# Attention scores of two rounds in one run of TensorE, and one pool of eight PSUM banks

## The chip, the cores and the metric

The kernel runs on one core of one Trainium2 chip. The metric is the device time of one execution in microseconds (us). Nine runs of the kernel before have a median of 1870.49 us (1860.73 to 1880.05).

A core has TensorE (matrix products; results go to PSUM), VectorE, ScalarE, GpSimd and SyncE, each with its own queue of instructions worked off in order. PSUM has eight banks; a bank holds 512 fp32 values on each of 128 partitions. In the profile the engines are called PE, DVE, ACT, POOL and SP; PEld is the loading of TensorE's stationary operand.

## The reference

One transformer block over x of shape (16, 512, 256): a layernorm, causal attention with 16 heads of 16 dimensions, a mixture of 32 experts of which each token uses 4, and a shared expert; all sums go onto x.

```python
xn = _layernorm(x)
q, k = _rope(xn @ Wq.T, xn @ Wk.T)                # 16 heads of 16
scores = einsum('bqhd,bkhd->bhqk', q, k) / sqrt(16)
attn = softmax(where(causal, -inf, scores))
att = einsum('bhqk,bkhd->bqhd', attn, v) @ Wo.T
topk = top_k(softmax(xn @ router_w.T + router_bias), 4)   # weights made to sum to 1
moe = sum over the 4 chosen experts of weight * down(silu(gate(xn)) * up(xn))
shared = silu(xn @ sgate.T) * (xn @ sup.T) @ sdown.T
out = x + att + moe + shared
```

## The kernel before

All engines follow one order that the program writes out by hand. The main loop (L1074) runs over **rounds** `r`. Sixteen batch items, two halves `p` of the heads and ten rounds each give 320 rounds; a second pass over the scores trails by `LAG` = 12 rounds, so that 332 rounds have scores. In each round the loop calls `cut` (L1087), then `scores` (L1089), then sends off finished stores, and then places other work: `fill` steps (shared expert, later the experts) by a running balance of estimated cost, with the round's fixed `events` between and behind them (projections of q, k and v, transposes, routing, the attention sums `values`, the output projection).

**The scores** are computed twice. The first pass (`sq`, queries times keys) only yields each row's maximum: VectorE adds the causal mask and takes the maximum in one instruction for each block and head (L835, into `top`). `maxima` (L861) later transposes these maxima and adds them to the queries, as two more rows of the contraction. The second pass (`sk`, keys times queries, 18 rows instead of 16) then yields scores that are already shifted; ScalarE takes the exponential (L843, into `pe`), GpSimd zeroes the triangle above the diagonal (`cut`, L849), and `values` (L870) multiplies `pe` with v.

A head's operands lie in its own strip of 32 partitions, so that four matmuls for four heads use four different row groups of the array and run side by side. Four heads `g` = 0..3 share one round pair: an even round does `sq` of heads 0 and 1 and `sk` of heads 2 and 3, the odd round after it the same block with the heads exchanged. Within a round the matmuls of `sq` and `sk` alternate (L825). Per head, every block entry of `BLOCKS_Q` and `BLOCKS_K` has 512 columns in all: 512, 384 + 128 or 256 + 256.

**PSUM:** `ps_q` and `ps_k` (L90, L91) hold one tile of two banks each, for `sq` and `sk`. The pool `psum` (L92) holds four tiles of one bank, which all other matmuls take in turn through `bank` (L145). A tile can be taken again when all that read it are done. So `sq` of a round waits for the maxima of the round before, and `sk` for its exponential.

**Other names** in the prediction, with their lines: `psgu` and `psd` are the two matmul stages of the shared expert (L246, L258), `pg` and `py` those of the routed experts (L656, L680), `pxt` the transpose of an expert's rows (L643). Behind `psgu` and `pg` stands `glu` (L276): tanh on ScalarE, then two VectorE instructions, the last reading of the bank. Behind `pg` come the small VectorE instructions `four`, `wrow` and `who` (L666 to L674). `plt` and `pr` (L423, L459) belong to routing: `choose` and `rank` put a chain of some twenty small VectorE instructions behind them, and ScalarE copies `pr` to `ranks` (L461) only after its exponential of `wt` (L442), which waits for that chain. `pqk` is the projection of q and k (L755), `po` the product with v (L875), `place` (L521) VectorE's work that finds the rows of the expert blocks.

**Stages:** rounds 0 to 33 compute the routing; 34 to 129 scatter rows to the experts' blocks, with shared-expert steps as fill; 130 to 301 run the expert blocks as fill; from 302 on sums are combined and stored.

Of the kernel before, what the change touches and what calls it, by code (L numbers as in the profile page):

```python
# [11 lines left out]
F32 = mybir.dt.float32  # L12
# [10 lines left out]
P = 128  # L23
# [49 lines left out]
def block_kernel(ctx: ExitStack, tc, x, wqkv, wo, rope, rw, rb, wexp, sg, su, sd, out):  # L73
# [16 lines left out]
    ps_q = ctx.enter_context(tc.tile_pool(name="ps_q", bufs=1, space=PSUM))  # L90
    ps_k = ctx.enter_context(tc.tile_pool(name="ps_k", bufs=1, space=PSUM))  # L91
    psum = ctx.enter_context(tc.tile_pool(name="psum", bufs=4, space=PSUM))  # L92
# [52 lines left out]
    def bank(shape, name):  # L145
        return psum.tile(shape, F32, tag="m", name=name)
# [77 lines left out]
    def shared_steps(b, i2, late, sums, xt=None):  # L224
# [27 lines left out]
        def down():  # L252
            hold["py"] = bank([P, 2, D], f"psd_{name}")
            down_half(0)

        def down_half(il):
            for m in range(HS // P):
                nc.tensor.matmul(  # L258
                    hold["py"][:, il, :], lhsT=hold["h"][:, m, il * P : (il + 1) * P],
                    rhs=sd_sb[:, m, :], start=(m == 0), stop=(m == HS // P - 1),  # L260
                )
            if il == 0 and late:
                hold["xr"], *parts = hold["parts"]
                for part in parts:
                    nc.vector.tensor_tensor(hold["xr"], hold["xr"], part, ALU.add)
            if il == 1:
                nc.vector.tensor_tensor(hold["xr"], hold["xr"], hold["py"], ALU.add)
                stores.append((half(out_v if late else moe_v[0], b, i2), hold["xr"]))
# [4 lines left out]
            [down, lambda: down_half(1)],  # L273
# [526 lines left out]
    def scores(r):  # L800

        jobs = []
        if r < ROUNDS:
            b, s = divmod(r, 20)
            p, s = divmod(s, 10)
            g0 = 0 if s % 2 == 0 else 2
            sq = ps_q.tile([P, 2, S], F32, tag="q", name=f"sq_{r}")
            jobs.append([
                (sq[:, h, col : col + (i + 1) * P],
                 qts[b][(g0 + h) * HP : (g0 + h) * HP + DH, 2 * p + c, i * P : (i + 1) * P],  # L810
                 kts[b][(g0 + h) * HP : (g0 + h) * HP + DH, 2 * p + c, : (i + 1) * P])
                for c, i, col in BLOCKS_Q[s // 2] for h in range(2)
            ])
        if r >= LAG:
            bk, sk = divmod(r - LAG, 20)
            pk, sk = divmod(sk, 10)
            k0 = 2 if sk % 2 == 0 else 0
            st = ps_k.tile([P, 2, S], F32, tag="k", name=f"sk_{r}")
            jobs.append([
                (st[:, h, col : col + S - k * P],  # L820
                 kts[bk][(k0 + h) * HP : (k0 + h) * HP + DH + 2, 2 * pk + c, k * P : (k + 1) * P],
                 qts[bk][(k0 + h) * HP : (k0 + h) * HP + DH + 2, 2 * pk + c, k * P :])
                for c, k, col in BLOCKS_K[sk // 2] for h in range(2)
            ])
        for n in range(max(len(job) for job in jobs)):  # L825
            for job in jobs:
                if n < len(job):
                    dst, lhsT, rhs = job[n]
                    nc.tensor.matmul(dst, lhsT=lhsT, rhs=rhs, start=True, stop=True)  # L829
        if r < ROUNDS:  # L830
            for c, i, col in BLOCKS_Q[s // 2]:
                n = (i + 1) * P
                for h in range(2):
                    at = (g0 + h) * HP + DH + c
                    nc.vector.tensor_tensor_reduce(  # L835
                        out=junk[:, :n], in0=sq[:, h, col : col + n], in1=causal[:, S - n :],
                        scale=1.0, scalar=LOWEST, op0=ALU.add, op1=ALU.max,
                        accum_out=top[p][i][:, at : at + 1],
                    )
        if r >= LAG:  # L840
            j = sk // 2
            pe = work.tile([P, 2, S], F32, tag="pe", name=f"pe_{r}", bufs=8)
            nc.scalar.activation(pe, st, AF.Exp, scale=DH ** -0.5)  # L843
            uncut.append((pe, j))
            pes[bk, pk, j, k0 // 2] = pe
# [3 lines left out]
    def cut():  # L849


        for pe, j in uncut:
            for _, _, col in BLOCKS_K[j]:
                diag = pe[:, :, col : col + P]
                nc.gpsimd.affine_select(  # L855
                    out=diag, in_=diag, compare_op=ALU.is_ge, fill=0.0, base=0,
                    pattern=[[0, 2], [1, P]], channel_multiplier=-1,
                )
        uncut.clear()
# [10 lines left out]
    def values(b, p, c):  # L870
        po = bank([P, S], f"po_{b}_{p}_{c}")
        for k in range(NT):
            j, col = PLACE_K[c, k]
            for g in range(4):
# [3 lines left out]
                    rhs=pes[b, p, j, g // 2][:, g % 2, col : col + S - k * P],  # L878
# [195 lines left out]
    for r in range(last):  # L1074
# [12 lines left out]
        cut()  # L1087
        if r < ROUNDS + LAG:
            scores(r)  # L1089
# [63 lines left out]
```

## Time and profile before

| | |
|---|---|
| median of nine runs | 1870.49 us |
| the profiled execution, time | 1871.53 us |
| the profiled execution, span of its instructions | 1869.8 us |
| mean granted TensorE clock | 0.976 |
| instructions in the profile | 37883 |
| DMA, mean rate | 186 GB/s |

All steps of the prediction are added to the profiled execution's own time, 1871.53 us; 1.7 us of it lie outside the span. It stands 1.0 us above the median.

The profile's "busy" counts an engine as busy while any instruction is under way. Where an engine idles, the profile names what ended the wait (the releaser). The chain of waits is followed back from the last instruction. Each fp32 matmul shows as two passes, each a weight load and a matmul record, so a matmul of 512 columns appears twice. The end of a matmul is modelled, so starts are safer to compare than ends.

### The profile page before, as it was taken

Reading aid. Unit: us, or ns where it says so; the run is one execution under the profiler, and the core shown is the slowest. Engines: PE = TensorE matmul, PEld = TensorE weight load, DVE = VectorE, ACT = ScalarE, POOL = GpSimd, SP = SyncE. Lnnn points to the kernel's source line nnn. Section 1 sums busy time; section 2 is a strip of 40 time slices with the busy share of each in tenths; the row PEclk is TensorE's granted clock in tenths of the full one; section 3 lists DMA queues with packets and bytes.
Section 4 is the critical chain, followed back from the end, with each engine's and each line's share of the span. In section 5 each row is a group of like instructions: output and inputs, shape, how many; then the busy total and the mean of one; then the engine's idle time right before and its main releaser. Section 6 shows DMA issues by size and latency. Waiting matters only on the chain.

```text
span 1869.8 us, 37883 instructions
## 1 busy us (share of the span) xinstructions
PE 1773.0 (95%) x13361; PEld 1255.4 (67%) x13361; DVE 1223.5 (65%) x4243; ACT 839.3 (45%) x1481; POOL 1013.2 (54%) x1338
## 2 busy tenths in 40 slices
PE   8999998989888899999999999999999999999898
PEld 6765665656555556677777777777777777777555
DVE  6888885655655655566666667566665756666585
ACT  3345532333333333345555555555555555555432
POOL 3333416667657677525565565656565665665421
PEclk9999999899989999999999999999999999999999
DMA  4454443435444343357989798898989889897498
GB/s 161 163 179 152 162 146 131 155 119 184 138 157 155 109 149 104 129 162 202 237 195 244 191 233 225 199 236 199 242 196 232 218 205 239 191 249 164 107 304 277
DMA packets 227518, 347.97 MB, mean 186 GB/s; under 512 B 22656, under 2 KB 165760, under 8 KB 227328
## 3 DMA queue, kind: packets, MB, share of 16 engines
q1 hardware_dynamic: 167424, 260.29, 44.0%
q0 software_dynamic: 55296, 76.86, 21.0%
q10 hardware_dynamic: 4608, 8.39, 1.3%
q8 instruction: 106, 1.74, 0.4%
q14 instruction: 84, 0.69, 0.1%
HBM read 218.12 MB, written 128.39 MB: 185 GB/s over the span
## 4 chain that ended last, share of the span: by engine, by line
PE 78%; DVE 13%; DMA 4%; issue 2%; another core or an unknown queue 1%; ACT 1%; SPq 1%; POOL 0%; DVEq 0%; ACTq 0%; POOLq 0%
PE sq L829 15%; PE pg L656 14%; PE psgu L246 9%; PE py L680 7%; PE po L875 7%; PE pqk L755 5%; PE psd L258 4%; DVE junk L835 4%; PE pxt L643 4%; PE pt L793 3%; PE pv L783 3%; PE pa L923 2%; PE pot L891 1%; PE sk L829 1%
## 5 line engine op out<-in xcount | busy, mean ns | idle before, releaser
L835 DVE CUSTOM_DVE_ANT_0 junk<-sq,causal 128x256 bf16<-128x256 f32 (+3 forms) x1024 | 501.6, 490 | 282.3 <-PE sk L829 176.4
L694 POOL DMA_INDIRECT moe<-yb,who x288 | 449.6, 1561 | 333.8 <-DMA moe<-yb,who 120.7
L843 ACT ACTIVATE pe<-sk 128x1024 f32<-128x1024 f32 x320 | 327.7, 1024 | 368.7 <-PE sk L829 324.5
L829 PE MATMUL sq<-kt,qt 16*128 16x384 f32 (+3 forms) x2048 | 375.9, 467 | 45.0 <-DVE top L835 41.0
L855 POOL TENSOR_SCALAR_AFFINE_SELECT pe<-pe 128x256 f32<-128x256 f32 x512 | 270.9, 681 | 246.8 <-ACT pe L843 234.5
L829 PE MATMUL sk<-qt,kt 18*128 18x512 f32 (+3 forms) x2048 | 375.6, 467 | 1.3 <-issue 1.3
L829 PEld LDWEIGHTS sq<-kt,qt 16*128 16x128 f32 x2048 | 178.0, 186 | 185.1 <-issue 65.4
L656 PEld LDWEIGHTS pg<-xbt,w 128*128 128x128 f32 x2304 | 272.2, 191 | 34.0 <-issue 16.6
L549 POOL DMA_INDIRECT xs<-rows,pos x256 | 250.4, 978 | 81.1 <-issue 80.2
L656 PE MATMUL pg<-xbt,w 128*128 128x128 f32 x2304 | 288.3, 278 | 0.2 <-ACT xbt L647 0.2
L829 PEld LDWEIGHTS sk<-qt,kt 18*128 18x128 f32 x2048 | 178.0, 186 | 10.1 <-issue 7.6
L281 DVE SCALAR_TENSOR_TENSOR gs_e<-th_e,pg 128x256 f32<-128x256 f32 x144 | 60.6, 421 | 164.5 <-ACT th_e L279 151.0
L875 PE MATMUL po<-pe,va 128*32 128x512 f32 (+3 forms) x2048 | 155.5, 443 | 5.7 <-POOL pe L855 4.5
L680 PE MATMUL py<-w,ht 128*128 128x256 f32 x576 | 153.4, 389 | 1.3 <-DVE four L666 0.9
L246 PE MATMUL psgu<-sxt,sg_sb 128*128 128x256 f32 x496 | 146.3, 419 | 2.3 <-issue 1.8
L688 ACT ACTIVATE yb<-py,wrow 128x256 f32<-128x256 f32 x288 | 121.0, 473 | 33.1 <-PE py L680 28.3
L246 PE MATMUL psgu<-sxt,su_sb 128*128 128x256 f32 x496 | 135.4, 397 | 0.3 <-issue 0.2
L258 PE MATMUL psd<-sd_sb,hs 128*128 128x256 f32 x512 | 130.9, 399 | 3.2 <-DVE hs L282 2.4
L875 PEld LDWEIGHTS po<-pe,va 128*32 128x32 f32 x2048 | 60.8, 111 | 108.2 <-issue 84.1
L755 PE MATMUL pqk<-wqkv_sb,axt 128*128 128x512 f32 x240 | 119.4, 622 | 4.5 <-issue 3.6
L246 PEld LDWEIGHTS psgu<-sxt,sg_sb 128*128 128x128 f32 x496 | 90.2, 199 | 49.6 <-issue 29.2
L279 ACT ACTIVATE th_e<-pg 128x256 f32<-128x256 f32 x144 | 55.2, 383 | 146.9 <-PE pg L656 135.8
(150 smaller groups left out, 2394.1 us busy)
## 6 DMA issues: line engine op xcount, KB each, us to landing
w<-in_wexp SPq DMA_DIRECT2D x288, 384.5 KB
xb<-xs SPq DMA_DIRECT2D x144, 265.0 KB
sum<-moe SPq DMA_DIRECT2D x48, 256.0 KB
xn_d<-xn SPq DMA_DIRECT2D x16, 530.0 KB
rows<-xn_d SPq DMA_DIRECT2D x16, 530.0 KB
xt_d<-xt ACTq DMA_DIRECT2D x32, 256.0 KB
sxt<-xt_d SPq DMA_DIRECT2D x31, 256.0 KB
xn<-in_x SPq DMA_DIRECT2D x15, 512.0 KB
```

What stands on the lines that cost most here:

```text
L246: nc.tensor.matmul(ps[:, u, :], lhsT=w[:, c, m * P : (m + 1) * P], rhs=hold["xt"][:, c, :], start=(c == 0), stop=(c == 1),)
L258: nc.tensor.matmul(hold["py"][:, il, :], lhsT=hold["h"][:, m, il * P : (il + 1) * P], rhs=sd_sb[:, m, :], start=(m == 0), stop=(m == HS // ...
L549: nc.gpsimd.indirect_dma_start(out=views[n % NVIEWS], out_offset=bass.IndirectOffsetOnAxis(ap=index, axis=0), in_=row, in_offset=None,)
L656: nc.tensor.matmul(pg[:, u, c * HB : (c + 1) * HB], lhsT=w[n][:, c, at : at + H], rhs=rows[:, dc, c * HB : (c + 1) * HB], start=(dc == 0), ...
L680: nc.tensor.matmul(py[:, c, :], lhsT=h[:, c * P : (c + 1) * P], rhs=w[n][:, c, 2 * D : 3 * D], start=True, stop=True,)
L694: nc.gpsimd.indirect_dma_start(out=moe[c], out_offset=bass.IndirectOffsetOnAxis(ap=at[:, c : c + 1], axis=0), in_=yb[:, c, :], in_offset=N ...
L755: nc.tensor.matmul(pqk, lhsT=axts[b][:, c, tok], rhs=wqkv_sb[:, c, : 2 * D], start=(c == 0), stop=(c == 1),)
L829: nc.tensor.matmul(dst, lhsT=lhsT, rhs=rhs, start=True, stop=True)
L835: nc.vector.tensor_tensor_reduce(out=junk[:, :n], in0=sq[:, h, col : col + n], in1=causal[:, S - n :], scale=1.0, scalar=LOWEST, op0=ALU.a ...
L843: nc.scalar.activation(pe, st, AF.Exp, scale=DH ** -0.5)
L855: nc.gpsimd.affine_select(out=diag, in_=diag, compare_op=ALU.is_ge, fill=0.0, base=0, pattern=[[0, 2], [1, P]], channel_multiplier=-1,)
L875: nc.tensor.matmul(po[g * HP : (g + 1) * HP, k * P :], lhsT=va[b % 2][k][:, 8 * p + 4 * c + g, :], rhs=pes[b, p, j, g // 2][:, g % 2, col ...
```

## The change

`scores` is called only in even rounds and does the work of two rounds: `sq` of all four heads, one bank for each head, then `sk` of all four heads, one bank each. All eight banks become one-tile slots of one pool; `Q_BANKS` (0 to 3) and `K_BANKS` (4 to 7) serve the scores, and the list `free_banks` says in which order the other work takes banks between two runs: Q0, K0, Q1, K1, K2, K3. K banks return to the end of the list, Q banks do not (`once`).

Directly behind the matmuls stand the exponentials and the row maxima of heads 0 and 1. Those of heads 2 and 3 are put off: the exponentials behind the first fill step, the maxima behind the second (or to the end of the round). An exponential now covers one head (512 columns) instead of two (1024), and a `cut` instruction four heads instead of two. The shared expert's `down` takes one bank and one VectorE addition for each half instead of one for both. The number and shapes of the matmuls and of the row maxima stay.

```diff
-    ps_q = ctx.enter_context(tc.tile_pool(name="ps_q", bufs=1, space=PSUM))
-    ps_k = ctx.enter_context(tc.tile_pool(name="ps_k", bufs=1, space=PSUM))
-    psum = ctx.enter_context(tc.tile_pool(name="psum", bufs=4, space=PSUM))
+    psum = ctx.enter_context(tc.tile_pool(name="psum", bufs=1, space=PSUM))
+    Q_BANKS, K_BANKS = range(4), range(4, 8)
+    free_banks = [*K_BANKS, *Q_BANKS]
+    once = set()
...
-    def bank(shape, name):
-        return psum.tile(shape, F32, tag="m", name=name)
+    def bank(shape, name, n=None):
+        if n is None:
+            n = free_banks.pop(0)
+            if n not in once:
+                free_banks.append(n)
+        return psum.tile(shape, F32, tag=f"bank{n}", name=name)
...
     def scores(r):
+        later = []
         if r < ROUNDS:
...
+            sq = [bank([P, S], f"sq_{r}_{g}", Q_BANKS[g]) for g in range(4)]
+            for c, i, col in BLOCKS_Q[s // 2]:
+                for g in range(4):
+                    nc.tensor.matmul(
+                        sq[g][:, col : col + (i + 1) * P],
...
         if r >= LAG:
...
+            st = [bank([P, S], f"sk_{r}_{g}", K_BANKS[g]) for g in range(4)]
+            for c, k, col in BLOCKS_K[sk // 2]:
+                for g in range(4):
...
+            pe = work.tile([P, 4, S], F32, tag="pe", name=f"pe_{r}", bufs=4)
+            def exponentials(heads):
+                for g in heads:
+                    nc.scalar.activation(pe[:, g, :], st[g], AF.Exp, scale=DH ** -0.5)
+            exponentials((0, 1))
+            later.append(lambda: exponentials((2, 3)))
...
+            row_maxima((0, 1))
+            later.append(lambda: row_maxima((2, 3)))
+        if r < ROUNDS:
+            free_banks[:] = [Q_BANKS[0], K_BANKS[0], Q_BANKS[1], *K_BANKS[1:]]
+            once.update(Q_BANKS)
+        else:
+            free_banks[:] = [*Q_BANKS, *K_BANKS]
+            once.clear()
+        return later
...
-        cut()
-        if r < ROUNDS + LAG:
-            scores(r)
+        if r % 2 == 0:
+            cut()
+            later = scores(r) if r < ROUNDS + LAG else []
...
             step()
             owed -= cost
+            if later:
+                later.pop(0)()
...
+        while later:
+            later.pop(0)()
```

More of the change, by code (lines that the diff above doesn't have):

```diff
@@ L250, in gate_up, with down @@
             glu(hold["h"][:, m, :], ps, f"s{name}_{m}")
[L252 to L256, printed above, removed]
+        def down(il):
+            py = bank([P, D], f"psd_{name}_{il}")
             for m in range(HS // P):
                 nc.tensor.matmul(
-                    hold["py"][:, il, :], lhsT=hold["h"][:, m, il * P : (il + 1) * P],
-                    rhs=sd_sb[:, m, :], start=(m == 0), stop=(m == HS // P - 1),
+                    py, lhsT=hold["h"][:, m, il * P : (il + 1) * P], rhs=sd_sb[:, m, :],
+                    start=(m == 0), stop=(m == HS // P - 1),
                 )
@@ L265, in down_half @@
                     nc.vector.tensor_tensor(hold["xr"], hold["xr"], part, ALU.add)
+            here = hold["xr"][:, il, :]
+            nc.vector.tensor_tensor(here, here, py, ALU.add)
             if il == 1:
-                nc.vector.tensor_tensor(hold["xr"], hold["xr"], hold["py"], ALU.add)
                 stores.append((half(out_v if late else moe_v[0], b, i2), hold["xr"]))
@@ L272, in shared_steps @@
             [lambda m=m: gate_up(m) for m in range(HS // P)],
-            [down, lambda: down_half(1)],
+            [lambda il=il: down(il) for il in range(2)],
         )
@@ L800, in scores @@
     def scores(r):
-        jobs = []
+        later = []
         if r < ROUNDS:
@@ L805, in scores @@
             p, s = divmod(s, 10)
[L806 to L813, printed above, removed]
+            sq = [bank([P, S], f"sq_{r}_{g}", Q_BANKS[g]) for g in range(4)]
[3 more added lines that the diff above has]
+                        sq[g][:, col : col + (i + 1) * P],
+                        lhsT=qts[b][g * HP : g * HP + DH, 2 * p + c, i * P : (i + 1) * P],
+                        rhs=kts[b][g * HP : g * HP + DH, 2 * p + c, : (i + 1) * P],
+                        start=True, stop=True,
+                    )
         if r >= LAG:
@@ L816, in scores @@
             pk, sk = divmod(sk, 10)
[L817 to L829, printed above, removed]
-        if r < ROUNDS:
[L831 to L845, printed above, removed]
+            st = [bank([P, S], f"sk_{r}_{g}", K_BANKS[g]) for g in range(4)]
+            for c, k, col in BLOCKS_K[sk // 2]:
+                for g in range(4):
+                    rows = slice(g * HP, g * HP + DH + 2)
+                    nc.tensor.matmul(
+                        st[g][:, col : col + S - k * P],
+                        lhsT=kts[bk][rows, 2 * pk + c, k * P : (k + 1) * P],
+                        rhs=qts[bk][rows, 2 * pk + c, k * P :],
+                        start=True, stop=True,
+                    )
@@ new lines, in scores, with row_maxima @@
+            pe = work.tile([P, 4, S], F32, tag="pe", name=f"pe_{r}", bufs=4)
[4 more added lines that the diff above has]
+            later.append(lambda: exponentials((2, 3)))
+            uncut.append((pe, sk // 2))
+            pes[bk, pk, sk // 2] = pe
+        if r < ROUNDS:
+            def row_maxima(heads):
+                for g in heads:
+                    for c, i, col in BLOCKS_Q[s // 2]:
+                        n = (i + 1) * P
+                        at = g * HP + DH + c
+                        nc.vector.tensor_tensor_reduce(
+                            out=junk[:, :n], in0=sq[g][:, col : col + n], in1=causal[:, S - n :],
+                            scale=1.0, scalar=LOWEST, op0=ALU.add, op1=ALU.max,
+                            accum_out=top[p][i][:, at : at + 1],
+                        )
+            row_maxima((0, 1))
+            later.append(lambda: row_maxima((2, 3)))
@@ L856, in cut @@
                     out=diag, in_=diag, compare_op=ALU.is_ge, fill=0.0, base=0,
-                    pattern=[[0, 2], [1, P]], channel_multiplier=-1,
+                    pattern=[[0, 4], [1, P]], channel_multiplier=-1,
                 )
@@ L877, in values @@
                     lhsT=va[b % 2][k][:, 8 * p + 4 * c + g, :],
-                    rhs=pes[b, p, j, g // 2][:, g % 2, col : col + S - k * P],
+                    rhs=pes[b, p, j][:, g, col : col + S - k * P],
                     start=(k == 0), stop=(k == NT - 1), skip_group_check=True,
```

## The prediction

> **What bounds the kernel now.** I read the page's busy times and groups first:
>
> ```profile
> PE 1773.0 (95%) x13361; PEld 1255.4 (67%) x13361; DVE 1223.5 (65%) x4243; ACT 839.3 (45%) x1481; POOL 1013.2 (54%) x1338
> PE 78%; DVE 13%; DMA 4%; issue 2%; another core or an unknown queue 1%; ACT 1%; SPq 1%; POOL 0%; DVEq 0%; ACTq 0%; POOLq 0%
> L829 PE MATMUL sq<-kt,qt 16*128 16x384 f32 (+3 forms) x2048 | 375.9, 467 | 45.0 <-DVE top L835 41.0
> ```
>
> PE sets the end. It idles 97 us, 45.0 of them ahead of `sq`, which waits for the maxima of the round before. Then by stage (rounds 0-33, 34-129, 130-301, 302-319); the columns are stretch, length, and busy time of PE, PEld, DVE, ACT and POOL, then clock, DMA share and GB/s:
>
> ```profile
> 32.60:263.30 230.70, 215.78 (x1474) 151.39 (x1473) 192.67 (x769) 101.31 (x219) 77.78 (x232) 0.96 0.47 155
> 263.30:798.10 534.80, 480.41 (x3182) 314.64 (x3180) 319.46 (x998) 172.57 (x261) 343.55 (x442) 0.94 0.43 142
> 798.10:1737.00 938.90, 935.49 (x7772) 697.28 (x7768) 605.58 (x2204) 510.50 (x921) 551.19 (x558) 1.00 0.84 211
> 1737.00:1808.50 71.50, 61.99 (x497) 38.32 (x496) 49.42 (x155) 27.48 (x39) 18.15 (x35) 0.98 0.66 195
> ```
>
> In the third stage, half of the time, PE has almost no gap: only less PE work helps there. In the first, DVE is 84% busy. Run by run on the timeline, the waits ahead of `sq` are 5.3, 34.1, 0.6 and 5.2 us in the four stages.
>
> What a run of scores costs PE, from the timeline of an undisturbed one:
>
> ```profile
> 600.25 1.89 PE L258 MATMUL psd<-sd_sb,hs 128*128 128x256 f32 x8
> 602.08 0.69 PE L829 MATMUL sq<-kt,qt 16*128 16x512 f32 x1
> 602.61 0.59 PE L829 MATMUL sq<-kt,qt 16*128 16x512 f32 x1
> 603.14 1.07 PE L875 MATMUL po<-pe,va 128*32 128x512 f32 x8
> ```
>
> Two passes of four heads side by side take 0.53 us each. Inside longer runs a pass starts 0.32 us after one of 384 columns, so 512 columns alone are 0.43. The first pass and the way out thus carry 0.10 us each. The start carries 0.10 too: `psd` and the run overlap by 0.06 us (602.14 against 602.08), where neighbours of one kind overlap by 0.16. A run costs 0.31 us above its 0.86 us of streaming, nearly the same in all undisturbed runs.
>
> **Part 1, half the runs.** 320 rounds with `sq` become 160 runs: 160 x 0.31 = **-50 us** (5, 15, 27 and 3 by stage). That assumes that `sq` to `sk` costs no more than block to block does now. The rule that weighs against it is in the Trainium skill, "TensorEngine Tiling (Array Packing)", PSUM Bottleneck: tiling makes TensorE faster but not the emptying of PSUM, which may become the bound. It has no price; part 3 prices that side from rows.
>
> **Part 2, the old wait.** `sq` no longer waits for maxima issued directly before: these get a whole cycle of some 11 us. **-40 us** (5.3 + 34.1 + 0.6; the fourth stage is left out, see part 5).
>
> **Part 3, the new wait.** The first tile taken after a run is Q0, the bank of `sq` head 0. PE works in order, so the first fill step, and all behind it, waits until DVE has done head 0's maxima. DVE works in order too, and what is left from the fill steps ahead of the run comes first. Call D the time from a run's first matmul to its first maximum. One run whose last fill step was `pg`:
>
> ```profile
> 1208.73 0.58 PE L829 MATMUL sq<-kt,qt 16*128 16x384 f32 x1
> 1209.31 0.42 DVE L281 SCALAR_TENSOR_TENSOR gs_e<-th_e,pg 128x256 f32<-128x256 f32 x1 [1.48 <-ACT th_e L279]
> 1209.76 0.42 DVE L282 SCALAR_TENSOR_TENSOR ht<-gs_e,pg 128x256 f32<-128x256 f32 x1
> 1210.10 0.91 DVE L666 SCALAR_TENSOR_TENSOR four<-xb,w 128x4 f32<-128x4 f32 x2
> 1211.28 0.54 DVE L835 CUSTOM_DVE_ANT_0 junk<-sq,causal 128x384 bf16<-128x384 f32 x1
> ```
>
> D is 2.55 us here, though the scores were there after 1.15. Head 0's maxima take 0.73 us (512 columns) to 0.93 (384 + 128), 0.85 in the mean, and PE follows 0.05 later, as ahead of `sq` now. Without the wait the fill would begin at 2 x 0.86 + 0.20 = 1.92 us. The wait is therefore D + 0.90 - 1.92 = **D - 1.02 us** a run. Its floor is 0.17, as no D is below 1.19.
>
> I took D of every even round, whose preceding steps the change keeps. Means by stage: 4.07 (17 runs), 2.71 (48), 1.51 (86), 1.41 (9); 2.14 over all.
>
> - Rounds 130-301: where `py` is the last step (30 runs) D is 1.22, where it is `pg` (23 runs) 2.09, a chain that the change leaves. 86 x 0.49 = **+42 us**.
> - Rounds 0-33: `choose` and `rank` stand last in odd rounds, so D is their chain:
>
> ```profile
> 141.29 0.48 PE L829 MATMUL sq<-kt,qt 16*128 16x256 f32 x1 [0.53 <-DVE top L835]
> 142.72 0.28 DVE L425 TENSOR_TENSOR lg<-plt,rb_sb 128x128 f32<-128x128 f32 x1
> 145.84 0.21 ACT L442 ACTIVATE wt<-wt 128x16 f32<-128x16 f32 x1 [2.92 <-DVE wt L439]
> 145.96 0.25 ACT L461 COPY ranks<-pr 128x128 f32<-128x128 f32 x1
> 146.93 0.41 DVE L835 CUSTOM_DVE_ANT_0 junk<-sq,causal 128x256 bf16<-128x256 f32 x1
> ```
>
>   D is 5.64. Before, the next round's work covered it; now PE stands. `pr` also holds a K bank until ScalarE copies it, 4.9 us into the run, so `sk` stands too, inside the same wait. 17 x 3.05 = **+52 us**. Of this stage's 9.6 us of other PE idle time I take back half, **-5**: some are waits behind the same chain.
> - Rounds 34-129: nine of the thirteen D above 3 stand behind an odd round that ends with `po`, 2 us of PE work that gives DVE nothing; what DVE still holds then is mostly the odd round's maxima (1.5 to 1.9 us), which now run earlier. I take 1.6 us for 32 runs, 2.5 where `place` falls in the even round (9 runs) and 3.0 where in the odd (7): mean 1.97, 48 x 0.95 = **+46 us**. Bounds: D = 1.5 gives 23, the whole 2.71 gives 81.
>
> Emptying the K banks ahead of `sk` costs nothing more while DVE is later. The second tile, K0, needs the exponential of head 0: some 0.6 us after `sk` (ScalarE's copies of 512 columns take 0.585). After a first step `pxt` (0.44 us) that is 0.15 late: 29 x 0.15 = **+4 us**. Should ScalarE be behind as well, this grows, at most by the 0.6 us in all 160 runs.
>
> **Part 4, the clock.** The longest wait of PE now shows what standing still costs (columns as above):
>
> ```profile
> 703.07 1.21 PE L829 MATMUL sq<-kt,qt 16*128 16x512 f32 x1 [3.98 <-DVE top L835]
> 702.00:703.00 1.00, 0.00 (x0) 0.00 (x0) 0.93 (x7) 0.00 (x0) 0.70 (x2) 0.79 0.37 136
> 703.00:704.00 1.00, 0.93 (x4) 0.52 (x8) 1.00 (x4) 0.00 (x0) 0.69 (x2) 0.50 0.17 59
> ```
>
> The clock fell to 0.50 and stayed there for 6 us, which cost 3.1 us; a stall of 3 us near 380 us cost 3.2 us at half clock, 1.6. Ten runs of the first stage have D above 4, so waits above 3 us: 10 x 1.6 = **+16 us**, up to 31. The Trainium skill, "TensorE: Matmul & The Clock Gate", Part 1, has the gate open again after some 3.4 us of work; by it the estimate would be 10 x 1.7 = 17 us, and the long case above contradicts it.
>
> **Part 5, the rest.** Two exponentials of 512 columns (at 0.585) stand for one of 1024 (1.024): 320 x 0.15 = 47 us more on ACT, which is 45% busy and idles 369 us ahead of them. Two additions of 256 columns behind `psd` (0.42 each, as `gs`) stand for one of 0.68: 32 x 0.16 = 5 us more on DVE, between fill steps. Without that cover both would be paid, 52 us. Half as many `cut` instructions of twice the width take POOL at most the 271 us they take now, and `po` waited only 4.5 us for them. The twelve rounds with `sk` alone become six runs (7 us less PE), and the nine waits of the fourth stage would be 9 x 0.39 = 4 us, but from 1785 us on the chain of waits goes through DMA (`sum` loads and stores): **0** here, between -7 and +4.
>
> **Sum:** -50 - 40 + 42 + 52 - 5 + 46 + 4 + 16 = +65, so 1871.5 + 65 = **1937 us**: by stage +53, -3, +18 and -3. The median stands 1 us below the profiled time, which I neglect.
>
> **Rivals.**
> 1. *DVE catches up* (faster). The odd round's maxima move ahead by half a round, and DVE starts each run with less behind it. Parts 1 to 3 balance at a mean D of 1.02 + 90 / 160 = 1.58 us (2.14 now); below it the kernel is faster. At 1.35: 160 x 0.33 - 90 = -37, **1834 us**. For: 47 of the 86 runs of the third stage have D under 1.25. Against: the chains behind `pg` and `rank` start only when PE ends the step, whatever DVE did before. Chance 0.13.
> 2. *No relief* (slower still). D in rounds 34-129 stays at 2.71 (+35) and the clock costs 3.1 us a wait (+15): **1987 us**, and more if K0 comes late. For: DVE-heavy bursts already cost 34 us there. Chance 0.17.
> 3. *The runs don't pay*: `sq` to `sk` drains the array as a change of kind does, and part 1 gives nothing, +50: 1987 us. Against: the block of 384 columns and the next of 128 follow each other without a gap now. Chance 0.04, in the range above.
> 4. *A wash*: relief in the second stage and short clock losses just balance, 1866 to 1877 us. Chance 0.06.
>
> The forecast, 1877 to 1975, has 0.60. Faster by over 0.3% (which is about what a measurement of this kernel tells from no change) 0.13, within it 0.06, slower 0.81. The range for eight in ten goes from 1866, leaving most of rival 1 out, to 1990.
>
> **What would show it.** Right: PE waits for DVE `top` in front of the first fill tiles (`psgu`, `pg`, `pxt`), some 0.5 us a run in the third stage and 3 us in the first; none ahead of `sq`; runs of 2.0 us; a first stage some 50 us longer with a lower clock. Wrong: waits there below 90 us in all, D in the first stage near 2, or PE waiting mainly for ACT or for a K bank ahead of `sk`.

## The result, and the profile after

The changed kernel takes 2087.53 us (median of 20 runs, 2077.03 to 2105.13); the kernel before, timed beside it, 1864.01 us (62 runs). The ratio is 1.1205, 95% interval 1.1183 to 1.1226: slower by 223.5 us, where +65 was forecast. The direction was right, the size far off, beyond the range's upper end of 1990.

The profiled execution (2085.22 us), from the page: busy times of the engines, the granted clock in 40 slices, the chain of waits, and the groups of the two score passes.

```profile
PE 1872.3 (90%) x13361; PEld 1356.3 (65%) x13361; DVE 1224.5 (59%) x4275; ACT 847.6 (41%) x1801; POOL 967.8 (46%) x1082
PEclk9888998888888889789999999999999999999999
PE 68%; DVE 18%; issue 4%; another core or an unknown queue 4%; DMA 3%; ACT 3%; SPq 0%; POOL 0%; DVEq 0%; ACTq 0%; POOLq 0%
L815 PE MATMUL sq<-kt,qt 16*128 16x128 f32 (+3 forms) x2048 | 228.1, 472 | 26.2 <-ACT oc L901 10.9
L828 PE MATMUL sk<-qt,kt 18*128 18x128 f32 (+3 forms) x2048 | 251.9, 471 | 36.7 <-ACT ranks L466 7.5
```

DVE does the work it did before, but holds 18% of the chain instead of 13%. PE is "busy" 99 us longer with the same matmuls, mostly because its clock is lower (86 of the 99, worked out below). By stage (rounds 0-33, 34-129, 130-301; columns as in the prediction):

```profile
32.90:316.80 283.90, 235.87 (x1473) 168.97 (x1473) 194.81 (x777) 102.81 (x239) 75.59 (x215) 0.87 0.38 126
316.80:958.80 642.00, 546.90 (x3186) 369.27 (x3184) 319.41 (x1015) 175.03 (x357) 326.00 (x365) 0.85 0.36 119
958.80:1947.80 989.00, 948.33 (x7772) 724.52 (x7768) 603.58 (x2205) 513.94 (x1093) 532.45 (x422) 0.99 0.80 201
```

Each stretch runs from the first `sq` matmul of its stage to that of the next. Against before they are longer by 53, 107 and 50 us, where +53, -3 and +18 were forecast. The first stage came out as worked; the second holds most of the miss. The waits, by waiting group and releaser (us in total, times, longest), first PE's, then ScalarE's and DVE's:

```profile
PE psgu L253 <- DVE top L850: 28.5, 15, 5.1
PE psd L262 <- DVE top L850: 17.5, 8, 5.1
PE pa L942 <- DVE qt L885: 13.7, 5, 4.4
PE sq L815 <- ACT oc L901: 10.9, 3, 5.0
ACT pe L838 <- remote: 69.6, 13, 8.8
ACT oc L901 <- remote: 43.2, 7, 9.8
DVE junk L850 <- remote: 29.4, 6, 7.4
```

The first two are the forecast wait for Q0. With all smaller ones, the waits for DVE `top` ahead of other tiles than `sq` come to 54 us, less than the 90 below which the prediction called itself wrong. The third and fourth were not forecast. "Remote" means that a release arrived just before the waiting instruction started, while no instruction ended then that could have sent it: in all these rows it is a release by PE. The same rows stand in the profile of before, and the prediction passed over them:

```profile
ACT oc L882 <- remote: 41.2, 7, 7.8
DVE junk L835 <- remote: 37.3, 8, 7.6
```

All of them lie in rounds 34 to 129. This is what one looks like in the changed kernel, on the timeline of round 90:

```profile
692.72 0.44 PE L894 MATMUL po<-pe,va 128*32 128x128 f32 x5 [0.82 <-issue]
694.18 0.38 PE L894 MATMUL po<-pe,va 128*32 128x128 f32 x2 [1.01 <-issue]
694.49 1.28 PE L815 MATMUL sq<-kt,qt 16*128 16x384 f32 x2
696.95 0.96 POOL L554 DMA_INDIRECT xs<-rows,pos  x1 [0.30 <-issue]
700.11 0.58 ACT L901 COPY oc<-po 128x512 f32<-128x512 f32 x1 [5.52 <-remote]
700.74 1.02 PE L815 MATMUL sq<-kt,qt 16*128 16x384 f32 x5 [4.98 <-ACT oc L901]
```

The last matmul of `po` is over by 694.6, yet ScalarE's copy of it starts at 700.11: it was released 5.5 us late. Before, `sq` and `sk` had banks of their own and went on meanwhile (behind a `po` for whose release ScalarE stood 7.8 us, PE waited 3.0, for the copy itself). Now `sq` needs the bank that `po` holds, and PE stands for 4.98 us. In two single microseconds behind it the core looks so (columns as by stage):

```profile
699.00:700.00 1.00, 0.00 (x0) 0.00 (x0) 0.00 (x0) 0.00 (x0) 0.00 (x0) 0.50 0.00 0
707.00:708.00 1.00, 1.00 (x3) 0.67 (x3) 0.00 (x0) 0.00 (x0) 0.84 (x3) 0.50 0.00 0
```

At 699 no engine and no DMA does anything; eight microseconds later PE still runs at half clock. Releases are not all that is late: inside `po`, at 692.72, PE stood for 0.82 us with no wait at all ("issue"). Such idle time of PE comes to 29.6 us in rounds 34 to 129, and to 16.1 in the kernel before.

### The profile page after: what moved, and what is told of

Same layout as the page of the kernel before. It is cut to its first block, busy times and chain, and to the rows that moved or that the text cites. A ratio compares the mean times of both kernels' runs of the same rounds, so it can differ in the third digit from the quotient of the medians.

```text
span 2083.5 us, 38577 instructions
## 1 busy us (share of the span) xinstructions
PE 1872.3 (90%) x13361; PEld 1356.3 (65%) x13361; DVE 1224.5 (59%) x4275; ACT 847.6 (41%) x1801; POOL 967.8 (46%) x1082
## 4 chain that ended last, share of the span: by engine, by line
PE 68%; DVE 18%; issue 4%; another core or an unknown queue 4%; DMA 3%; ACT 3%; SPq 0%; POOL 0%; DVEq 0%; ACTq 0%; POOLq 0%
PE psgu L253 11%; PE pg L661 11%; PE sk L828 7%; PE po L894 6%; PE sq L815 6%; PE psd L262 5%; PE py L685 5%; DVE junk L850 5%; PE pqk L760 4%; PE pa L942 3%; PE pxt L648 3%; PE pt L798 3%; PE pv L788 2%; DMA moe<-yb,who 2%
## 5 line engine op out<-in xcount | busy, mean ns | idle before, releaser
L850 DVE CUSTOM_DVE_ANT_0 junk<-sq,causal 128x384 bf16<-128x384 f32 (+3 forms) x1024 | 501.6, 490 | 247.2 <-PE sq L815 115.8
L838 ACT ACTIVATE pe<-sk 128x512 f32<-128x512 f32 x640 | 347.1, 600 | 353.7 <-PE sk L828 252.2
L874 POOL TENSOR_SCALAR_AFFINE_SELECT pe<-pe 128x512 f32<-128x512 f32 x256 | 196.2, 878 | 360.4 <-ACT pe L838 168.4
L828 PE MATMUL sk<-qt,kt 18*128 18x128 f32 (+3 forms) x2048 | 251.9, 471 | 36.7 <-ACT ranks L466 7.5
L815 PE MATMUL sq<-kt,qt 16*128 16x128 f32 (+3 forms) x2048 | 228.1, 472 | 26.2 <-ACT oc L901 10.9
L828 PEld LDWEIGHTS sk<-qt,kt 18*128 18x128 f32 x2048 | 139.8, 196 | 111.9 <-issue 40.8
L815 PEld LDWEIGHTS sq<-kt,qt 16*128 16x128 f32 x2048 | 108.8, 188 | 104.8 <-issue 41.5
L286 DVE SCALAR_TENSOR_TENSOR gs_s<-th_s,psgu 128x256 f32<-128x256 f32 x128 | 53.5, 418 | 187.7 <-ACT th_s L284 168.3
L284 ACT ACTIVATE th_s<-psgu 128x256 f32<-128x256 f32 x128 | 49.1, 384 | 274.0 <-PE psgu L253 231.0
L262 PEld LDWEIGHTS psd<-sd_sb,hs 128*128 128x128 f32 x512 | 113.0, 228 | 64.9 <-DVE top L850 25.4
```

The source lines that it names most:

```text
L262: nc.tensor.matmul(py, lhsT=hold["h"][:, m, il * P : (il + 1) * P], rhs=sd_sb[:, m, :], start=(m == 0), stop=(m == HS // P - 1),)
L815: nc.tensor.matmul(sq[g][:, col : col + (i + 1) * P], lhsT=qts[b][g * HP : g * HP + DH, 2 * p + c, i * P : (i + 1) * P], rhs=kts[b][g * HP ...
L828: nc.tensor.matmul(st[g][:, col : col + S - k * P], lhsT=kts[bk][rows, 2 * pk + c, k * P : (k + 1) * P], rhs=qts[bk][rows, 2 * pk + c, k * ...
L838: nc.scalar.activation(pe[:, g, :], st[g], AF.Exp, scale=DH ** -0.5)
L850: nc.vector.tensor_tensor_reduce(out=junk[:, :n], in0=sq[g][:, col : col + n], in1=causal[:, S - n :], scale=1.0, scalar=LOWEST, op0=ALU.a ...
L874: nc.gpsimd.affine_select(out=diag, in_=diag, compare_op=ALU.is_ge, fill=0.0, base=0, pattern=[[0, 4], [1, P]], channel_multiplier=-1,)
```

## The experiments

Theory A is the prediction's: PE stands behind each run until DVE has done head 0's maxima. Theory B: a run takes all eight banks, so whatever still empties one of the last fill tiles stops it. Theory C: the late releases come from the indirect scatters of rounds 36 to 129. Later a fourth cause came up, the put-off itself.

The runs fell on five chips (e1 to e4, e5 to e8, e9 to e12, e13 to e16, e17 and e18), and that proved to matter: each ratio is to the kernel before on the same chip. Differences between runs of different chips, given below where nothing better exists, are weaker.

| run | before | this | ratio (95% interval) |
|---|---|---|---|
| e1 before, no maxima | 1869.98 | 1829.26 | 0.9762 (0.9684 to 0.9839) |
| e2 after, no maxima | 1869.98 | 1963.26 | 1.0482 (1.0428 to 1.0536) |
| e3 K banks only, sq then sk | 1869.98 | 2169.62 | 1.1587 (1.1536 to 1.1638) |
| e4 K banks only, sk then sq | 1869.98 | 2230.89 | 1.1956 (1.1871 to 1.2041) |
| e5 pm in the odd round | 1865.47 | 2065.95 | 1.1109 (1.1018 to 1.1200) |
| e6 nothing put off | 1865.47 | 2016.26 | 1.0824 (1.0737 to 1.0910) |
| e7 after, plain scatter | 1865.47 | 1961.36 | 1.0531 (1.0448 to 1.0614) |
| e8 before, plain scatter | 1865.47 | 1804.72 | 0.9692 (0.9613 to 0.9771) |
| e9 odd rounds' events first | 1803.36 | 1981.30 | 1.0991 (1.0951 to 1.1030) |
| e10 nothing put off, pm odd | 1803.36 | 1887.42 | 1.0480 (1.0446 to 1.0514) |
| e11 after, no maxima, plain scatter | 1803.36 | 1802.67 | 0.9993 (0.9974 to 1.0012) |
| e12 before, no maxima, plain scatter | 1803.36 | 1757.11 | 0.9748 (0.9713 to 0.9784) |
| e13 after, unaltered | 1802.81 | 1961.79 | 1.0884 (1.0849 to 1.0919) |
| e14 nothing put off | 1802.81 | 1883.74 | 1.0442 (1.0404 to 1.0481) |
| e15 as e14, routing early | 1802.81 | 1859.05 | 1.0320 (1.0285 to 1.0354) |
| e16 before, side parts | 1802.81 | 1803.68 | 0.9999 (0.9971 to 1.0028) |
| e17 exponentials not put off | 1808.41 | 1934.43 | 1.0686 (1.0651 to 1.0721) |
| e18 maxima not put off | 1808.41 | 1889.55 | 1.0450 (1.0428 to 1.0473) |

### Without the maxima: e1, e2

```diff
             for c, i, col in BLOCKS_Q[s // 2]:
...
-                nc.vector.tensor_tensor_reduce(
...
+                pass
```

> The kernel before without its row maxima (the maxima stay zero, so the softmax is not shifted; everything else runs). PE's 45 us ahead of the first pass should go and DVE should lose some 290 us of work. Both theories: about 1820 to 1835 us. It is the control for the next run.

> The changed kernel without its row maxima, so that no bank is ever held for them. Theory A (the first tile behind a run waits for DVE's maxima, and nothing else matters): the waits behind the runs and the clock lost through them go, and what is left is the kernel without maxima, less 50 us for half the runs: 1775 to 1800 us. Theory B (a run needs all eight banks at once, so whatever still holds a bank of the last fill tile, ScalarE's copy or DVE's reading of it, stops PE): rounds 34 to 129 stay above 590 us and the total above 1880 us.

e1 came as expected. e2 did not fall to 1800: 134 us of the 223 stay with no maxima at all, and rounds 34 to 129 take 604.9 us. So theory A is not the whole; e2 lies where theory B put it, but so would theory C.

### Fill in the K banks alone: e3, e4

```diff
-            exponentials((0, 1))
-            later.append(lambda: exponentials((2, 3)))
+            exponentials(range(4))
...
-            free_banks[:] = [Q_BANKS[0], K_BANKS[0], Q_BANKS[1], *K_BANKS[1:]]
+            free_banks[:] = [*K_BANKS]
```

In e4 the block that issues `sk` also stands ahead of the one that issues `sq`.

> The changed kernel with fill tiles in the four K banks alone; the Q banks are lent no more, and the four exponentials stand directly behind the run. Fill then never waits for maxima, but its first tile waits for the exponential of head 0, some 0.7 us behind the run: 160 x 0.7 = 112 us of waits. Theory A: 1871 - 50 - 40 + 112 = about 1890 us, and in rounds 34 to 129 about 535 + 20 = 555 us. Theory B: the second pass still waits for the last fill tile, but the first pass has its own banks and covers 1 us of that: rounds 34 to 129 at 580 to 620 us, the total at 1930 to 1980 us.

> As the run before, but the second pass (sk) comes first in a run and the first pass (sq) behind it, so that the exponential of head 0 is done when the run ends. Theory A: no wait is left behind a run, 1871 - 50 - 40 = about 1785 us, up to 1820. Theory B: the run now begins with the pass that needs the banks of the last fill tiles, and PE stands each time until they are emptied, 1 to 2 us in most of 160 runs: 1950 to 2080 us.

Both theories were far off: the two kernels are 82 and 143 us slower than the changed one, not faster. The wait behind the run in e3 is the one worked out (in rounds 130 to 301 fill starts 2.68 us after the run does at the earliest, 0.75 above the undisturbed 1.93), but with two banks fewer later fill tiles wait as well: that stage took 1058 us, against 989. So not lending the Q banks is worse than lending them, and the test does not separate A from B.

### pm a round later, nothing put off, and both: e5, e6, e10

```diff
-        at(r + 10, 0.45, lambda b=b, p=p: maxima(b, p))
+        at(r + 11, 0.45, lambda b=b, p=p: maxima(b, p))
```

```diff
-            exponentials((0, 1))
-            later.append(lambda: exponentials((2, 3)))
+            exponentials(range(4))
...
-            row_maxima((0, 1))
-            later.append(lambda: row_maxima((2, 3)))
+            row_maxima(range(4))
```

> The changed kernel with the step that adds the maxima to the queries (pm and its addition qt) moved from the even round to the odd round behind it, so that no run's maxima of heads 0 to 3 are queued between. If the waits at the seventh and eighth tile behind a run in rounds 130 to 301 (29 us more than before) come from qt standing behind the even round's maxima, that stage falls from 989 to about 965 us and the total to about 2060 us. Rival: qt is late through the glu chain alone; then the stage stays within 5 us and the total at 2080 to 2095.

> The changed kernel with exponentials and maxima of all four heads directly behind the run. The glu of the first fill steps then stands behind 3.4 us of maxima instead of 1.7, but K1 to K3 are free earlier. Theory A (DVE behind the run is what counts): 30 to 60 us longer than the changed kernel, 2115 to 2145 us. Theory B (what counts is that the last fill tiles are emptied before the run): within 15 us of it, 2072 to 2102 us, since nothing changes ahead of a run.

> The changed kernel with both gains found so far: nothing put off (2016 us alone) and pm in the odd round (2066 alone). If both remove the same wait (qt behind late maxima), the two together give little over the first: 2005 to 2020 us. If the put-off costs something else (DVE's idle time during the run, filled with the maxima, is lost when they are put off), they add up: about 1995 us.

e5: the total came out as expected, and rounds 130 to 301 fell from 989 to 974 us, some 60% of what was expected there. Rounds 34 to 129 fell as well (642 to 626), which was not expected. e6 contradicts both theories: DVE has twice as many maxima directly behind the run, and the kernel gains 71 us. e10 ran on another chip (below); against its own kernel before it is no better than e14, the same kernel without the first edit (1.0480 against 1.0442). That fits two edits that remove the same wait. The expected times hold for the chips of e1 to e8 and are not comparable.

### Plain instead of indirect scatters: e7, e8, e11, e12

```diff
-            nc.gpsimd.indirect_dma_start(
-                out=views[n % NVIEWS],
-                out_offset=bass.IndirectOffsetOnAxis(ap=index, axis=0),
-                in_=row,
-                in_offset=None,
-            )
+            nc.gpsimd.dma_start(views[n % NVIEWS][done[0] * HB : (done[0] + 1) * HB, :], row)
+            done[0] += 1
```

> The changed kernel with the 288 indirect scatters of rounds 36 to 129 replaced by plain transfers of the same rows from the same queue to consecutive places (the expert blocks then get rows of other experts, whose weight is zero). In the profile, ScalarE's copy oc and DVE start up to 6.6 us after the last matmul of po in rounds 34 to 129 only. Theory C (the indirect transfers of that stage hold up the semaphore updates of PE): these waits vanish, rounds 34 to 129 fall from 642 to 560 to 600 us, total 2005 to 2045. Rival: the lag belongs to po or to the number of transfers; it stays, rounds 34 to 129 within 15 us of 642, total 2070 to 2095.

> The kernel before with the same replacement, as its control. Theory C: rounds 34 to 129 fall from 535 us to 490 to 515, total 1825 to 1850. Rival: within 8 us, total 1862 to 1878.

These kernels leave out that a row lands in the block of its expert, so their output is not the block's; the number and the sizes of the transfers stay. Every "remote" wait vanishes in both profiles, and with them PE's "issue" time in rounds 34 to 129. The changed kernel gains 126 us, the kernel before 61, more than expected; rounds 34 to 129 fall to 518.3 and 467.5. So the late releases hang on the indirect transfers there, and they cost the changed kernel twice as much.

> The changed kernel without row maxima and with plain scatters, to see what is left when both are gone. Theory B: runs still wait for the emptying of the last fill tiles; rounds 34 to 129 take 490 to 505 us and rounds 130 to 301 stay at 943, the total at 1860 to 1885. If maxima and late releases were the whole, the new runs' gain would now show: 1720 to 1760 us.

> The kernel before without row maxima and with plain scatters, as the control of the run before. Rounds 34 to 129 at 450 to 462 us, total 1765 to 1785; under theory B it stays 80 to 110 us faster than the run before.

What is left with maxima and late releases both gone is 45.6 us, half of what theory B asked for. The profiles differ by less, 36 us (that of e11 is its fastest run): 33 in the first stage, 7 in the second, and the third is 5 us faster. There theory B can be seen, in e11 with no maxima at all:

```profile
974.79 2.02 PE L657 MATMUL pg<-xbt,w 128*128 128x128 f32 x16 [0.33 <-PE py L681]
976.75 1.15 PE L811 MATMUL sq<-kt,qt 16*128 16x256 f32 x16
977.33 0.42 DVE L286 SCALAR_TENSOR_TENSOR gs_e<-th_e,pg 128x256 f32<-128x256 f32 x1 [2.09 <-ACT th_e L284]
977.72 1.77 PE L824 MATMUL sk<-qt,kt 18*128 18x256 f32 x16
977.79 0.42 DVE L287 SCALAR_TENSOR_TENSOR ht<-gs_e,pg 128x256 f32<-128x256 f32 x1
979.42 0.66 PE L644 MATMUL pxt<-ident,xb 128*128 128x128 f32 x4
```

`sk` starts at 977.72, 0.97 after `sq`, but lasts 1.77 instead of some 1.1 us: one of its heads needs the bank of `pg`, which `ht` frees at 978.2. Fill follows 2.67 us after the run's start instead of 1.93. This chain is the one that sets D behind `pg`, which is why leaving out the maxima alone takes little from such a run: behind `pg`, fill follows after 2.83 us in the changed kernel and after 2.67 in e11, in the mean of 23 runs.

### po not last before a run: e9

```diff
         todo = list(events.get(r, []))
+        while r % 2 and todo:
+            todo.pop(0)[1]()
```

> The changed kernel with the fixed events of odd rounds (among them po) issued ahead of that round's fill steps, so that po is no longer the last tile before a run. Theory B: the run's wait for ScalarE's copy oc of that tile is then covered by fill; rounds 34 to 129 fall from 642 to 600 to 625 us, the total to 2045 to 2070. Theory A: what DVE holds ahead of a run grows, as fill with its glu now stands last; 2085 to 2120 us.

It is slower than the unaltered kernel on a chip with the same time before (1.0991 against 1.0884, about 19 us). With releases in time, `po` is no bad last tile, as ScalarE empties it in 0.6 us. Beside e13, rounds 34 to 129 take 15 us longer and rounds 130 to 301 17; that fill steps with their glu are the worse last tiles is likely, but not shown, as D in rounds 34 to 129 is the same (2.22 and 2.21). The first stage gains 13 us: the edit also moves `choose` and `rank` away from the run, and D falls there from 3.86 to 2.46. The expectations of both theories were written for a chip with late releases, which this one is not, so the run decides nothing between them.

### The same kernel on a chip without late releases: e13, e14

In e9 to e12 the kernel before took 1803 us, 62 to 67 less than in e1 to e8, and no wait was "remote", with indirect scatters too.

> The changed kernel, unaltered. In the last four runs the kernel before took 1803 us instead of 1865, and their profiles show no late releases in rounds 34 to 129 although the scatters were indirect in two of them. Theory C' (whether the releases come late belongs to the chip): where the kernel before takes about 1803 us, this one takes 1950 to 1975, as with plain scatters, and its profile shows no wait of ScalarE or DVE for a late release; where the kernel before takes about 1865, this one takes 2075 to 2100 with them. Rival (no such link): 2075 to 2100 us in either case.

> The changed kernel with nothing put off, on the same chip as the run before. If the 71 us it gained come from the put-off alone and not from the chip, it is 55 to 75 us faster than that run; if they came from fewer late releases, under 35 us where there are none.

e13: 1961.79 us, as expected. It matches e7 within 1 us, and the kernel before on this chip matches e8. At the place shown above (round 90) the copy follows `po` at once and `sq` never stops:

```profile
624.09 2.36 PE L894 MATMUL po<-pe,va 128*32 128x512 f32 x32
626.38 1.37 PE L815 MATMUL sq<-kt,qt 16*128 16x384 f32 x7
626.52 0.58 ACT L901 COPY oc<-po 128x512 f32<-128x512 f32 x1 [1.94 <-PE po L894]
```

In none of the ten profiles of e9 to e18, eight of them with indirect scatters, does such a wait show; each of the six of e1 to e6 has 19 or more. So these waits go with the chip, and the indirect scatter is needed for them. Each chip was measured at one time only: whether it is the chip or the state that it was in then stays open.

e14: 78 us faster than e13, a little more than expected; the put-off costs as much without late releases as with them (71, e6). The two timelines of DVE at the same place (round 180, `sq` starting at 1115.95 and at 1064.83) show how it costs. First e13:

```profile
1119.97 0.42 DVE L914 TENSOR_TENSOR ot<-pot,rs 128x256 f32<-128x256 f32 x1
1121.94 0.42 DVE L286 SCALAR_TENSOR_TENSOR gs_e<-th_e,pg 128x256 f32<-128x256 f32 x1 [1.54 <-ACT th_e L284]
1122.40 0.42 DVE L287 SCALAR_TENSOR_TENSOR ht<-gs_e,pg 128x256 f32<-128x256 f32 x1
1124.60 0.54 DVE L850 CUSTOM_DVE_ANT_0 junk<-sq,causal 128x384 bf16<-128x384 f32 x1
1126.33 1.22 DVE L885 TENSOR_TENSOR qt<-qt,pm 128x1024 f32<-128x1024 f32 x1
1127.60 1.32 PE L942 MATMUL pa<-wo_sb,oT 128*128 128x256 f32 x3 [4.43 <-DVE qt L885]
```

DVE idles 1.54 us waiting for `pg`'s tanh, while the scores of heads 2 and 3 have long been there; their maxima are queued behind it. They start at 1124.60, `qt` stands behind them, and PE waits 4.43 us for the bank of `pm`. (Between 1122.74 and 1124.60 stand `four`, `wrow` and `who`, which here took 1.3 us longer than in e14; now and then they do so in both kernels, so the example shows somewhat more than the mean.) In e14:

```profile
1069.73 0.29 DVE L849 CUSTOM_DVE_ANT_0 junk<-sq,causal 128x128 bf16<-128x128 f32 x1
1070.24 0.42 DVE L912 TENSOR_TENSOR ot<-pot,rs 128x256 f32<-128x256 f32 x1
1070.82 0.42 DVE L286 SCALAR_TENSOR_TENSOR gs_e<-th_e,pg 128x256 f32<-128x256 f32 x1 [0.16 <-ACT th_e L284]
1072.15 1.21 DVE L883 TENSOR_TENSOR qt<-qt,pm 128x1024 f32<-128x1024 f32 x1
1073.42 0.48 PE L940 MATMUL pa<-wo_sb,oT 128*128 128x256 f32 x1 [1.37 <-DVE qt L883]
```

All eight maxima are over when the tanh comes; they used the time in which DVE has nothing else. The same PE work waits 1.37 us. Over rounds 130 to 301, PE's waits for `qt` are 21.7 us in e13 and 6.1 in e14.

### Which half of the put-off: e17, e18

e17 keeps `row_maxima((0, 1))` and the put-off of `row_maxima((2, 3))`, with `exponentials(range(4))`; e18 the other way round.

> The changed kernel with all four exponentials directly behind the run; the maxima of heads 2 and 3 stay put off (now behind the first fill step, as they come first in the list). If the put-off costs through DVE (maxima of heads 2 and 3 queued behind the glu of fill steps, so that the next waits of PE for DVE grow), this gains little: 0 to 25 us against the changed kernel. If it costs through ScalarE (K2 and K3 emptied late), it gains 50 to 78 us.

> The changed kernel with all four heads' maxima directly behind the run; the exponentials of heads 2 and 3 stay behind the first fill step. The other half of the run before: 50 to 78 us gained if the put-off costs through DVE, 0 to 25 if through ScalarE; the two gains should add up to some 71 to 78.

e18 gains the whole (1.0450, beside 1.0442 for e14 and 1.0884 for e13): the maxima cost it. e17 gains more than expected, 0.020 or 36 us; it also moves the maxima from behind the second fill step to behind the first, so it is no clean test of the exponentials, and the two gains overlap.

### Routing a round earlier, and the side parts: e15, e16

```diff
-                at(2 * (it - 2) + k, cost, step)
+                at(max(0, 2 * (it - 2) + k - 1), cost, step)
```

```diff
-            nc.scalar.activation(pe, st, AF.Exp, scale=DH ** -0.5)
+            for h in range(2):
+                nc.scalar.activation(pe[:, h, :], st[:, h, :], AF.Exp, scale=DH ** -0.5)
```

e16 also has the changed kernel's `down`.

> As the run before, with all routing steps one round earlier, so that choose and rank stand in even rounds, a whole round ahead of a run. Theory: the first stage's loss is the chain of choose and rank that stands directly ahead of a run (it holds up the maxima and, through the copy ranks, a K bank); the first stage falls from 283 to 235 to 250 us, the total by 30 to 45 us. Rival: DVE is simply too busy there, the wait moves to another place; under 10 us.

> The kernel before with the side parts of the change alone: an exponential for each head (512 columns) instead of two heads, and a bank and an addition for each half behind psd. The prediction costed these at nothing; if so within 6 us of the kernel before, and if ScalarE or DVE have no room for them up to 50 us slower.

e15 gained 25 us, between the two expectations: in the first stage D fell from 3.94 to 2.24 us, but the stage only from 281 to 263. The chain of `choose` and `rank` ahead of the run is a third of the loss there (18 of 55 us), not all of it. e16 is no different from the kernel before; it leaves the wider `cut` out. e15 is the best version with two rounds in a run, and still 56 us slower than the kernel before on its chip; no run points to one that beats both.

## Why the prediction was wrong

The whole difference, in three pieces: without late releases and with nothing put off the change costs 81 us (e14, 1883.74 - 1802.81); the put-off adds 78 (e13 - e14); the late releases add 64.5 (223.5 on the chips that have them, 159.0 on one that has not; e7 and e8, on one chip, give 156.6 without them). The forecast was 65. Of the 81, 46 stay without any maxima (e11 - e12), where theory A has nothing left to wait for; the other 35 go with the maxima.

By stage, from the profiles: the two middle columns without late releases, against e16 as the kernel before; the last one the changed kernel against the kernel before, both with them:

| rounds | forecast | e14 - e16 | e13 - e16 | with late releases |
|---|---|---|---|---|
| 0-33 | +53 | +55 | +58 | +53 |
| 34-129 | -3 | +4 | +50 | +107 |
| 130-301 | +18 | +15 | +37 | +50 |
| from 302 on | -3 | +4 | +3 | +3 |

The third stage of the kernel before took 939 to 947 us in its several profiles, so a few us there mean nothing. The profiled run of e13 is its fastest and that of e14 its slowest, so their columns differ by some 70 us where the medians differ by 78. The e14 column can be read from its stretches beside those of the changed kernel above (e16: 225.9, 468.8 and 946.9):

```profile
34.50:315.60 281.10, 235.28 (x1474) 169.31 (x1474) 197.45 (x777) 103.42 (x239) 75.76 (x215) 0.87 0.38 128
315.60:788.80 473.20, 454.54 (x3184) 315.69 (x3182) 323.62 (x1015) 174.77 (x357) 328.60 (x365) 0.96 0.49 161
788.80:1750.60 961.80, 938.85 (x7773) 720.67 (x7769) 613.40 (x2205) 517.37 (x1093) 531.83 (x421) 0.99 0.83 206
```

The second stage of e13 and that of e16 beside them:

```profile
316.40:834.70 518.30, 488.71 (x3185) 335.25 (x3183) 318.36 (x1015) 174.84 (x357) 327.37 (x365) 0.92 0.44 147
258.20:727.00 468.80, 448.57 (x3186) 301.52 (x3184) 323.00 (x1015) 180.14 (x357) 344.37 (x442) 0.98 0.49 160
```

**The step that failed** is D of rounds 34 to 129, in the prediction's words: "what DVE still holds then is mostly the odd round's maxima (1.5 to 1.9 us), which now run earlier". It took D as 1.97. At 3.50 its own formula gives 48 x (3.50 - 1.02) = 119 us instead of 46; these 73 us more, and 49 of half clock that it did not price there, are more than the 110 by which the stage missed. Measured in the same way, by the start of each even round's first maximum, the means of that stage are:

| | with late releases | without |
|---|---|---|
| kernel before | 2.71 | 1.47 (e16) |
| changed kernel | 3.50 | 2.21 (e13) |
| nothing put off | 3.23 (e6) | 1.66 (e14) |

Two things are wrong in the sentence.
- After `po`, DVE did not hold maxima. It waited for PE's release: in all nine runs that the prediction counted, DVE stood idle for 1.8 to 7.3 us directly ahead of the first maximum, three times in the row of `junk` and "remote" shown above. Round 90 of the kernel before, whose `sq` started at 580.03, is one of them:

```profile
586.73 0.56 DVE L835 CUSTOM_DVE_ANT_0 junk<-sq,causal 128x384 bf16<-128x384 f32 x1 [7.31 <-remote]
```

Behind `po` the mean D of 14 runs is 4.03 us in the kernel before and 1.32 in e16. All that D of before had above 1.47 us (1.48 in e8) went with the late releases, so there was no backlog of maxima that could shrink. In the changed kernel the releases add 1.29 us to the mean D of 48 runs, 62 us, and a wait that only a bank of `sq` or `sk` sees, as in round 90, comes beside that.

- The maxima do not all run earlier. Those of heads 2 and 3 are put off behind the second fill step and its glu. The change says so, and the prediction gave the put-off no cost. It adds 0.55 us to D (2.21 - 1.66), 26 us in 48 runs, and 20 us at half clock; together the 45 us by which that stage differs. In rounds 130 to 301 it leaves D alone (1.48 and 1.47) and costs 22 us, 16 of them in PE's waits for `qt`, and with it for `pm`'s bank.

Rival 2 ("no relief", D stays at 2.71) came nearest, but D rose. Rival 1 put the balance at a mean D of 1.58; e15 has 1.60 and is 56 us slower, so D alone does not price a run that needs all eight banks.

**The other steps.**
- Part 1: an undisturbed run is 1.93 us (0.97 from `sq` to `sk`) as worked out, and rival 3 falls. But one run in eight of rounds 34 to 129 and one in twenty of rounds 130 to 301 was undisturbed in the changed kernel, and the third stage of e11 is only 5 us shorter than that of e12, where 27 were due: waiting for the eight banks took most of the gain back. The Trainium skill, "TensorEngine Tiling (Array Packing)", PSUM Bottleneck, which the prediction quoted against the change, says that the copies out of PSUM may become the bottleneck; these waits agree.
- Part 2: `sq` waits 4.9 us for maxima instead of 41.0, as forecast; it took on waits for the last fill tiles instead (`oc` 10.9).
- Part 3, first stage: +53 forecast and measured, and e15 confirms the chain of `choose` and `rank` as a cause. That the number agrees is in part luck, as the wait for maxima is not the whole of it: 33 us stay there without any maxima (e11 against e12). PE idles 20 us more in e11, 8.4 of it for `ranks`, which holds the K bank of `pr`, and half clock costs 16 more. Third stage: D was 1.49 (1.51 taken), and fill began 41 us later in all than behind undisturbed runs, where 42 were forecast.
- "Emptying the K banks ahead of `sk` costs nothing more while DVE is later" held where both hang on the same chain, behind `pg`, and failed where the emptying is late by itself, behind a `po` with a late release.
- Part 4: half clock cost 128 us in the changed kernel and 42 before (PE's busy time at half clock, halved): +86, not +16 to +31. In the first stage, the only one priced, it was +22; +49 fell in the second. Without late releases and put-off it is +45.
- Part 5: nothing, as forecast (e16), for the exponentials and the additions.
- The put-off of the maxima is no term of the sum: the prediction set it at nothing without a reason, and it measured 78 us.

What stays open is why the indirect scatters hold up PE and its releases on some chips and not on others.

## What to carry to other kernels

Work that is put off is priced by what it is put behind: on an engine that works in order, maxima that could fill an idle gap cost 78 us once they were queued behind a step that waits for another engine. A row of "remote" waits in the profile of before is lateness that the schedule hides in part, and a change that makes tiles share banks exposes more of it: it cost the kernel before 61 us and the changed kernel 126. And a kernel that runs on another chip should be compared there: 62 of 1865 us came and went with the chip.

## What the runs showed of the hardware

- In the changed kernel ScalarE and DVE stood up to 9.8 us for releases of PE that came late (5.5 us after the matmul in round 90), in rounds 34 to 129 alone; so they did in e1 to e6. With plain transfers instead of indirect ones (e7, e8, on the chip of e5 and e6), or on the chips of e9 to e18, they never did. The indirect additions to `moe` in rounds 130 to 301 show no such wait.
- The spells of half clock last 3.41 us or a multiple: in e14 17 of one unit, 11 of two, 1 of three; in the changed kernel 28 of its 49 last two, and the longest five. The Trainium skill, "TensorE: Matmul & The Clock Gate", Part 1, gives a free-running window of 3413 ns; the traces agree, as all spells of one execution begin on one grid of 3.41 us. But PE, back at work at 700.74, got its full clock only at 708.54, after two whole windows of work.
- In these traces it depends on the work. Take the windows of 3.41 us at half clock in which PE was busy throughout, 652 in the 20 traces. Where `sq` and `sk`, which use 16 or 18 rows, filled less than 20% of the window, the next one had the full clock 515 times of 515; where they filled 45% or more, it stayed at half 71 times of 71; in between it went either way. In round 90 they filled 83% of the first window and none of the second. So a long run of scores directly behind a stall goes with a longer half clock; no run was made to test this alone.
